# Cross-attention on one core: 64-row products in pairs, mask and maximum in one pass, longer load steps, last keys in 256 columns

## The chip, the cores and the metric

The kernel runs on one core of one Trainium2 chip. The metric is the device time of one execution in microseconds. The core has five engines with a queue each: TensorE (PE; PEld is its weight load), VectorE (DVE), ScalarE (ACT), GpSimd (POOL) and SyncE (SP), which here only issues DMAs. The engines wait for each other through semaphores.

## What is computed

Sixteen batches of 256 query rows attend to 77 keys each with 8 heads; then come an output projection, a residual and a layer norm. The reference, cut:

```python
Q = (img_embed @ Wq).reshape(B, -1, H, D).transpose(0, 2, 1, 3)     # B=16, 256 rows, H=8, D=256
K = (sent_embed @ Wk).reshape(B, -1, H, D).transpose(0, 2, 1, 3)    # 77 keys of 192 features
V = (sent_embed @ Wv).reshape(B, -1, H, D).transpose(0, 2, 1, 3)
score = jnp.einsum('bhqd,bhkd->bhqk', Q, K) / math.sqrt(D)
score = jnp.where(mask, score, -jnp.inf)
attn = jax.nn.softmax(score, axis=-1)
ctx = jnp.einsum('bhqk,bhkd->bqhd', attn, V).reshape(B, -1, H * D)
out = ctx @ Wo + img_embed
return (out - mu) * jax.lax.rsqrt(var + EPS) * gamma + beta
```

All inputs but the integer mask are 32-bit floats.

## The kernel before

**Folded weights.** The kernel multiplies the weights first: `gA` and `gB` hold Wq times Wk for each head, `uA` and `uB` hold Wv times Wo. The 192 features of the keys are split into 128 (the A part) and 64 (the B part). So each later product with the keys has two parts: A, a product over 128 rows, and B, over 64 rows, where two products can share the array, one in its upper and one in its lower half. Both parts add up in the same PSUM bank.

**Tiles.** A tile `t` is 128 query rows, so batch `b` has tiles 2b and 2b+1. Four batches (8 tiles) are a group `g`. x is held by group (`xg`), beside a copy `xT` whose 32 by 32 blocks VectorE turns after the load (L147 to L150).

**The loop.** `for b in range(-1, B - 1)` (L882 on) is software-pipelined: a pass works on the scores of batch b+1 and on the output of batch b, and finishes the norm of batch b-1. I call one turn of it a pass. In the order in which a pass is written:

- `scores` (L276) of the two new tiles: 128 products of 154 columns into four PSUM banks.
- `shift` (L292) of each: VectorE adds the mask's bias to the scores of eight heads (L298, two instructions) and takes the negative maximum per head (L305).
- `prepare_vw` (L198) makes batch b+1's keys times `uA`, `uB` in two banks `pv`; `prepare_a` (L153) makes one quarter of the next group's keys times `gA`, `gB` in four banks `pa`. All A parts are issued first (L208, L173), then all B parts (L219, L185). For the last group half of the batches are done at a time, with 154 columns instead of 308.
- `exponential` (L308): sixteen ACTIVATEs on ScalarE, one per head and tile, with the head's maximum as bias. `finish` takes the norm's statistics of an old tile. `weigh` (L315): VectorE sums the exponentials (L318) and inverts the sums (L320), POOL multiplies (L326) into `p`.
- ScalarE copies `pv` and `pa` from PSUM into `vw` and `a` (L922), POOL forms differences of `vw` (L379).
- `seven` (L402): seven block products instead of eight, in two banks `pm` and `po`, through `contract` (L413). The last 13 keys of each of the eight heads are a product of their own (`last`, L427), taken in columns of 128.
- VectorE normalises an old tile (L513, L532), turns the new `p` (L336), and on some passes `xT`. At the end of the pass come loads for the next group, `add_seven` (POOL and VectorE add the products to x) and `sums` (POOL, four additions on the turned `p` that the next `seven` uses).

From pass 13 on, `attend` (L343) takes the place of `seven`, and the last tiles are finished after the loop.

**What sets the order.** The kernel writes out the order of each engine's queue by hand (`manual_schedule`), so the order above is the order on each engine. All PSUM tiles share one ring of eight banks (`ps_mm`, `bufs=8`): the ninth tile asked for takes the bank of the first and waits for whoever reads that last. A pass asks for twelve: four for scores, two `pv`, four `pa`, two for `seven`. Each engine works its queue in order; an instruction that waits holds all behind it.

Of the kernel before, what the change touches and what calls it, by code (L numbers as in the profile page):

```python
# [1 line left out]

# [9 lines left out]
ALU = mybir.AluOpType  # L12
# [8 lines left out]
KM = 64  # L21
MASKED = 3.0e38


@with_exitstack
def kernel(
# [84 lines left out]

    def load_x(g):
        xg_of[g] = const.tile([P, GT, DI], F32, tag=f"xg{g}", name=f"xg_{g}")
        nc.sync.dma_start(xg_of[g], x_rows[:, g * GT : (g + 1) * GT, :])

# [36 lines left out]

    def prepare_a(g, places, lo=0, hi=GB):  # L153


        if 0 in places:
            a_of[g] = in_two("a", [P, 2, GB, H, S2], g)
        parts = [
            (2 * u + i, dc) for u in places for dc in range(2) for i in range(2)
        ]  # L160
        batches = slice(g * GB + lo, g * GB + hi)
        banks = [
            ps_mm.tile([P, hi - lo, S2], F32, tag="mm", name=f"pa_{g}_{h}_{dc}_{lo}")
            for h, dc in parts
        ]

        def cols(dc, i):
            return slice((2 * i + dc) * BK, (2 * i + dc + 1) * BK)

        def part_A():  # L170
            for (h, dc), o in zip(parts, banks):
                for i in range(NM):
                    nc.tensor.matmul(  # L173
                        flat(o[i * BK : (i + 1) * BK]),
                        gA[:, h, cols(dc, i)],
                        flat(cA[:, batches, :]),
                        start=True,
                        stop=False,
                    )

        def part_B():
            for j in range(0, len(parts), 2):
                for i in range(NM):
                    for k, (h, dc) in enumerate(parts[j : j + 2]):
                        nc.tensor.matmul(  # L185
                            flat(banks[j + k][i * BK : (i + 1) * BK]),
                            gB[half(k), h // 2, cols(dc, i)],
                            flat(cB[half(k), batches, :]),
                            start=False,
                            stop=True,  # L190
                        )

        def copies():
            return [(a_of[g][:, dc, lo:hi, h, :], o) for (h, dc), o in zip(parts, banks)]

        return part_A, part_B, copies

    def prepare_vw(b):  # L198

        vw_of[b] = vwp.tile([P, 4, 2, P], F32, tag="vw", name=f"vw_{b}", bufs=3)  # L200
        parts = slice(0, 4) if b < NS else slice(1, 5)
        pv = []

        def part_A():
            for k in range(2):
                pv.append(ps_mm.tile([P, 2 * DI], F32, tag="mm", name=f"pv_{b}_{k}"))
                for i in range(NM):
# [3 lines left out]
                        uA[:, parts, :, i],  # L211
                        start=True,
                        stop=False,
                    )

        def part_B():
            for i in range(NM):
                for k in range(2):
# [3 lines left out]
                        uB[half(k), parts, :, i],  # L222
                        start=False,
                        stop=True,
                    )
# [66 lines left out]
    def shift(t):  # L292
# [3 lines left out]
        s = sp.tile([P, H, S2], F32, tag="s", name=f"s_{t}")  # L296
        for a in range(2):
            nc.vector.tensor_tensor(  # L298
                s[:, a * H // 2 : (a + 1) * H // 2],
                ps[a][:, : H // 2 * S2].rearrange("p (h k) -> p h k", k=S2),  # L300
                bias[:, b, :].unsqueeze(1).to_broadcast([P, H // 2, S2]),
                ALU.add,
            )
        top = st.tile([P, H], F32, tag="top", name=f"top_{t}")
        nc.vector.tensor_reduce(top, s, AX.X, ALU.max, negate=True)  # L305
        s_of[t] = s, top

    def exponential(t):  # L308
        e = sp.tile([P, H, S2], F32, tag="e", name=f"e_{t}")
        s, top = s_of.pop(t)  # L310
        for h in range(H):
            nc.scalar.activation(e[:, h], s[:, h], AF.Exp, bias=top[:, h : h + 1])  # L312
        e_of[t] = e

    def weigh(t):  # L315
        e = e_of.pop(t)
        den = st.tile([P, H], F32, tag="den", name=f"den_{t}")
        nc.vector.tensor_reduce(den, e, AX.X, ALU.add)  # L318
        rden = st.tile([P, H], F32, tag="rden", name=f"rden_{t}")
# [82 lines left out]
    def seven(b):  # L402
# [7 lines left out]
        s1, s3, s2, s4 = (ss[:, i] for i in range(4))  # L410
        ends = vr[:, b, :P], vr[:, b, P:]

        def contract(out, *terms):  # L413
            for n, (weight, moving) in enumerate(terms):
                for i in range(NM):
# [3 lines left out]
                        moving,  # L419
                        start=(n == 0),  # L420
                        stop=(n == len(terms) - 1),
                    )
# [3 lines left out]

        last = [(pT[i][:, NF], vr[:, b, j * P : (j + 1) * P]) for i in range(QT) for j in range(2)]  # L427
        contract(pm[:, 0], *block(pT[0][:, 0:2], b11))
        contract(pm[:, 1], *block(s2, t2))
        contract(pm[:, 2], *block(s3, t3))  # L430
        contract(pm[:, 3], *block(s1, t1))
        contract(po[:, 0], *block(pT[0][:, 2:4], b21), last[0])
        contract(po[:, 1], *block(s4, b22), last[1])
        contract(po[:, 2], *block(pT[1][:, 2:4], t4), last[2])
        contract(po[:, 3], last[3])
        for i in range(QT):
# [441 lines left out]


    assert QT == 2  # L880
    last = NT - 1
    for b in range(-1, B - 1):  # L882
# [12 lines left out]
        for t in new:  # L895
            shift(t)
        for n in range(0, 2) if b < 0 else range(b + 2, min(b + 3, B // 2)):
            turn_last(n)
        g, n = (b + 1) // GB + 1, (b + 1) % GB
        work = [prepare_vw(b + 1)]  # L900
        if g < NG - 1 or g == NG - 1 and n < NF // 2:
            work.append(prepare_a(g, (n,)))
        elif b < NS:
            work.append(prepare_a(NG - 1, (NF // 2 + n % 2,), *((0, 2) if g < NG else (2, GB))))
        for part_A, _, _ in work:
            part_A()
        for _, part_B, _ in work:
            part_B()
        for i, t in enumerate(new):
# [3 lines left out]
            weigh(t)  # L913
        if old and b < B - 2:
            spread(old[0], old[-1] + 1)
        if b < 0:
            bias_of(GB, B)
            for j in range(GT // 2, GT, 2):
                transpose_x(0, j)
        for _, _, copies in work:  # L920
            for dst, src in copies():
                nc.scalar.copy(dst, src)  # L922
        if b + 1 < NS:
            differences(b + 1)
        if b < NS:
# [5 lines left out]
            for t in new:  # L931
                turn(t)
            if g < NG and n >= NF - 2:
                for j in range((n - NF + 2) * GT // 2, (n - NF + 3) * GT // 2, 2):
                    transpose_x(g, j)
            if old:
                normalise(old[1])


            if g < NG and n == NF - 1:  # L940
                load_x(g)
            elif g < NG and n:
                load_xT(g, (n - 1) * GT // 2, n * GT // 2)
            if now:
                add_seven(b)
            if b + 1 < NS:
                sums(b + 1)
# [73 lines left out]
```

## Time and profile before

| | us |
|---|---|
| median of 3 runs (274.39 to 274.52) | 274.43 |
| the profiled execution | 274.61 |
| its span, from first to last instruction | 272.8 |
| loop's scores begin on TensorE | 53.3 |
| TensorE's last product ends | 268.1 |
| one pass, batches 2 to 9 | 14.10 |
| busy in the pass 120.05 to 134.15: TensorE / VectorE / ScalarE / POOL | 14.10 / 11.86 / 7.65 / 10.94 |

The profiled execution is one execution, so differences are counted against its span; what lies outside the span is the same small amount in each. The chain of waits follows the last instruction back to whatever released it; a wait off that chain costs nothing until it becomes late. In rows of instructions, the number behind x is how many there are, and "mean ns" is how long one takes from its start to its end; neighbours on an engine may overlap, so the distance from start to start can be shorter. TensorE's products overlap too, and their ends are modelled: their starts are what to compare. A few rows of VectorE, ScalarE and POOL that the change touches:

```profile
L312 ACT ACTIVATE e<-s,top 128x77 f32<-128x77 f32 x256 | 66.8, 346 | 73.4 <-DVE top L305 73.4
L298 DVE TENSOR_TENSOR s<-ps,bias 128x308 f32<-128x308 f32 x64 | 29.7, 473 | 14.7 <-PE ps L283 14.6
L318 DVE TENSOR_REDUCE den<-e 128x8 f32<-128x616 f32 x32 | 24.9, 777 | 5.1 <-ACT e L312 4.9
L305 DVE TENSOR_REDUCE top<-s 128x8 f32<-128x616 f32 x32 | 25.4, 795 | 1.1
```

### The profile page before, as it was taken

What the parts mean: (1) busy time and instruction counts of PE and PEld (TensorE: products, weight loads), DVE (VectorE), ACT (ScalarE), POOL (GpSimd) and SP (SyncE); (2) the same over time, 40 slices, a digit from 0 to 9 for tenths busy, and PEclk for the clock granted to TensorE, in tenths of its full rate; (3) what the DMA queues carried; (4) which work ended last, traced back from release to release, by engine and by line L of the source; (5) the groups of instructions that cost most, each with busy time, mean ns of one, the idle gap of its engine ahead of it and who ended that gap; (6) DMA issues with size and microseconds to landing.
All of it is one profiled execution on the core that took longest, in us unless ns stands there. A gap on an engine that the chain in (4) does not pass through costs nothing.

```text
span 272.8 us, 14124 instructions
## 1 busy us (share of the span) xinstructions
PE 265.8 (97%) x6312; PEld 194.3 (71%) x6312; DVE 214.1 (78%) x418; ACT 136.2 (50%) x444; POOL 170.4 (62%) x231
## 2 busy tenths in 40 slices
PE   7999999999999999999999999999999999999992
PEld 6557486867494949495959586867796969694662
DVE  0554938589759898979799897878798989889875
ACT  3233225363918182827364646464546372927652
POOL 1000002809887878687878777777788789845754
PEclk9999999999999999999999999999999999999999
DMA  6999989940000322310221405000504061010102
GB/s 191 194 198 189 305 160 183 278 53 2 2 5 4 88 35 73 124 44 4 70 52 36 87 19 180 31 16 9 116 2 120 2 197 41 5 43 4 61 22 77
DMA packets 42460, 22.66 MB, mean 83 GB/s; under 512 B 23632, under 2 KB 41632, under 8 KB 42400
## 3 DMA queue, kind: packets, MB, share of 16 engines
q1 hardware_dynamic: 42400, 21.77, 34.8%
q8 instruction: 49, 0.80, 1.3%
q14 instruction: 11, 0.09, 0.1%
HBM read 17.57 MB, written 4.19 MB: 80 GB/s over the span
## 4 chain that ended last, share of the span: by engine, by line
PE 89%; DMA 7%; DVE 1%; SPq 1%; issue 0%; DVEq 0%
PE ps L283 25%; PE pa L173 11%; PE po L416 10%; PE pv L208 10%; PE pm L416 9%; PE pv L219 6%; PE pa L185 5%; DMA wq_blk<-in_L_xattn_Wq_dram 5%; PE po L348 4%; PE pu L717 3%; PE pr L242 2%; DMA c_sb<-in_ctx_dram 2%; PE pw L731 1%; PE pr L254 1%; PE po L364 1%; PE pgb L777 1%
## 5 line engine op out<-in xcount | busy, mean ns | idle before, releaser
L312 ACT ACTIVATE e<-s,top 128x77 f32<-128x77 f32 x256 | 66.8, 346 | 73.4 <-DVE top L305 73.4
L283 PE MATMUL ps<-a,xT 128*32 128x154 f32 x2048 | 70.0, 294 | 0.0
L326 POOL TENSOR_TENSOR p<-e,rden 128x512 f32<-128x512 f32 x64 | 47.8, 768 | 31.8 <-DVE rden L320 16.6
L283 PEld LDWEIGHTS ps<-a,xT 128*32 128x32 f32 x2048 | 66.0, 110 | 1.5 <-issue 0.8
L298 DVE TENSOR_TENSOR s<-ps,bias 128x308 f32<-128x308 f32 x64 | 29.7, 473 | 14.7 <-PE ps L283 14.6
L449 POOL TENSOR_TENSOR xg<-xg,m 128x256 f32<-128x256 f32 x39 | 28.6, 733 | 12.8 <-DVE xg L463 10.7
L173 PE MATMUL pa<-cA,gA 128*32 128x308 f32 (+1 forms) x576 | 36.4, 394 | 0.0
L173 PEld LDWEIGHTS pa<-cA,gA 128*32 128x32 f32 x576 | 18.4, 110 | 20.3 <-issue 9.1
L208 PE MATMUL pv<-uA,cA 128*32 128x512 f32 x256 | 30.4, 592 | 0.0
L318 DVE TENSOR_REDUCE den<-e 128x8 f32<-128x616 f32 x32 | 24.9, 777 | 5.1 <-ACT e L312 4.9
L305 DVE TENSOR_REDUCE top<-s 128x8 f32<-128x616 f32 x32 | 25.4, 795 | 1.1
L336 DVE STREAM_TRANSPOSE pT<-p 128x640 f32<-128x640 f32 x32 | 25.1, 813 | 0.9 <-POOL p L326 0.9
L379 POOL TENSOR_TENSOR ts<-vw 128x768 f32<-128x768 f32 x13 | 23.9, 1839 | 0.0
L532 DVE SCALAR_TENSOR_TENSOR xg<-xg,rstd,bet 128x256 f32<-128x256 f32 x26 | 20.9, 803 | 1.9
L185 PE MATMUL pa<-cB,gB 64*32 64x308 f32 (+1 forms) x576 | 20.3, 392 | 0.0
L922 ACT COPY vw<-pv 128x512 f32<-128x512 f32 x32 | 17.1, 584 | 6.3 <-PE pv L219 6.3
L185 PEld LDWEIGHTS pa<-cB,gB 64*32 64x32 f32 x576 | 10.7, 107 | 12.3 <-issue 9.2
L594 POOL COPY cRA<-cA 128x208 f32<-128x208 f32 x1 | 0.4, 358 | 29.8 <-DVE cA L593 29.8
L416 PE MATMUL po<-vr,pT 128*32 128x128 f32 x416 | 18.5, 273 | 0.0
L922 ACT COPY a<-pa 128x308 f32<-128x308 f32 (+1 forms) x56 | 17.5, 416 | 0.0
L219 PE MATMUL pv<-uB,cB 64*32 64x512 f32 x256 | 17.4, 601 | 0.0
L463 DVE TENSOR_TENSOR xg<-po,xg 128x256 f32<-128x256 f32 x31 | 11.7, 415 | 5.0 <-PE po L416 4.6
(117 smaller groups left out, 408.7 us busy)
## 6 DMA issues: line engine op xcount, KB each, us to landing
xT<-in_x_dram SPq DMA_DIRECT2D x32, 128.0 KB, 4.4
xg<-in_x_dram SPq DMA_DIRECT2D x4, 1024.0 KB, 6.7
out_dram<-xg SPq DMA_DIRECT2D x11, 256.0 KB, 2.8
wo<-in_L_xattn_Wo_dram SPq DMA_DIRECT2D x4, 512.0 KB, 6.2
wq_blk<-in_L_xattn_Wq_dram SPq DMA_DIRECT2D x12, 128.0 KB, 4.7
wvT<-in_L_xattn_Wv_dram SPq DMA_DIRECT2D x16, 96.0 KB, 3.6
out_dram<-xg SPq DMA_DIRECT2D x10, 128.0 KB, 1.7
wk_blk<-in_L_xattn_Wk_dram SPq DMA_DIRECT2D x12, 96.0 KB, 4.6
```

Of the source, the lines that this page charges most:

```text
L173: nc.tensor.matmul(flat(o[i * BK : (i + 1) * BK]), gA[:, h, cols(dc, i)], flat(cA[:, batches, :]), start=True, stop=False,)
L185: nc.tensor.matmul(flat(banks[j + k][i * BK : (i + 1) * BK]), gB[half(k), h // 2, cols(dc, i)], flat(cB[half(k), batches, :]), start=False ...
L208: nc.tensor.matmul(pv[k][i * BK : (i + 1) * BK], cA[:, b, k * BK : (k + 1) * BK], uA[:, parts, :, i], start=True, stop=False,)
L219: nc.tensor.matmul(pv[k][i * BK : (i + 1) * BK], cB[half(k), b, k * BK : (k + 1) * BK], uB[half(k), parts, :, i], start=False, stop=True,)
L283: nc.tensor.matmul(ps[m // 2][i * BK : (i + 1) * BK, m % 2 * 2 * S2 : (m % 2 + 1) * 2 * S2], xT_of[g][:, j * NM + m, dc], flat(a_of[g][:, ...
L298: nc.vector.tensor_tensor(s[:, a * H // 2 : (a + 1) * H // 2], ps[a][:, : H // 2 * S2].rearrange("p (h k) -> p h k", k=S2), bias[:, b, :]. ...
L305: nc.vector.tensor_reduce(top, s, AX.X, ALU.max, negate=True)
L312: nc.scalar.activation(e[:, h], s[:, h], AF.Exp, bias=top[:, h : h + 1])
L326: nc.gpsimd.tensor_tensor(part, e_mh[:, :, :, keys], rden_mh.unsqueeze(3).to_broadcast(list(part.shape)), ALU.mult,)
L416: nc.tensor.matmul(out[i * BK : (i + 1) * BK], weight[:, i], moving, start=(n == 0), stop=(n == len(terms) - 1),)
L449: nc.gpsimd.tensor_tensor(to, to, what, ALU.add)
L922: nc.scalar.copy(dst, src)
```

## The change

Five edits are made together.

1. **64-row products in pairs.** For batches 0 to 11, two batches' preparations are issued in one pass (those with b+1 even): A and B of the first, then, after ScalarE's copies of the first in the program's order, B and A of the second. The next pass issues none. To this end the start and stop flags of the accumulation can be swapped (`rest_first`). Batches 12 to 15 are prepared one a pass, as before. For the half-group preparations two `pa` now share a bank.
2. **Mask and maximum in one pass.** `shift` becomes one instruction per head that adds the bias, writes the negated sum and its minimum; the exponential gets the scale -1. For the first 26 tiles ScalarE's exponential also gives the sum over the keys (`accum_out`), and VectorE's sum L318 is left out.
3. **Loads.** x and its turned copy are loaded in steps of four tiles at the head of passes with n even; before, x came in one step of eight tiles and the turned copy in two of four at the ends of passes.
4. **Order.** Turning xT and normalising the second old tile are put off, in the passes without preparation, to after the next pass's `shift`. In the passes with two, `sums` goes ahead of `add_seven`. In pass -1, turning the rest of group 0's xT and the bias of batches 4 to 15 move behind the turn of `p`.
5. **Last keys.** Their product is taken first in each half of `po`, in 256 columns.

```diff
-    def prepare_a(g, places, lo=0, hi=GB):
+    def prepare_a(g, places, lo=0, hi=GB, rest_first=False):
...
+        opening, closing = range(len(whole)), range(len(parts) - len(whole), len(parts))
...
-                        start=True,
-                        stop=False,
+                        start=not rest_first and n in opening,
+                        stop=rest_first and n in closing,
...
-        for a in range(2):
-            nc.vector.tensor_tensor(
-                s[:, a * H // 2 : (a + 1) * H // 2],
-                ps[a][:, : H // 2 * S2].rearrange("p (h k) -> p h k", k=S2),
-                bias[:, b, :].unsqueeze(1).to_broadcast([P, H // 2, S2]),
-                ALU.add,
+        top = st.tile([P, H], F32, tag="top", name=f"top_{t}")
+        for h in range(H):
+            a, k = divmod(h, H // 2)
+            nc.vector.tensor_tensor_reduce(
+                s[:, h],
+                ps[a][:, k * S2 : (k + 1) * S2],
+                bias[:, b, :],
+                scale=-1.0,
+                scalar=FAR,
+                op0=ALU.add,
+                op1=ALU.min,
+                accum_out=top[:, h : h + 1],
             )
-        top = st.tile([P, H], F32, tag="top", name=f"top_{t}")
-        nc.vector.tensor_reduce(top, s, AX.X, ALU.max, negate=True)
...
-            nc.scalar.activation(e[:, h], s[:, h], AF.Exp, bias=top[:, h : h + 1])
+            one = slice(h, h + 1)
+            nc.scalar.activation(
+                e[:, h],
+                s[:, h],
+                AF.Exp,
+                bias=top[:, one],
+                scale=-1.0,
+                accum_out=den[:, one] if t < QT * NS else None,
+            )
...
-        nc.vector.tensor_reduce(den, e, AX.X, ALU.add)
+        if t >= QT * NS:
+            nc.vector.tensor_reduce(den, e, AX.X, ALU.add)
...
-        contract(po[:, 0], *block(pT[0][:, 2:4], b21), last[0])
-        contract(po[:, 1], *block(s4, b22), last[1])
-        contract(po[:, 2], *block(pT[1][:, 2:4], t4), last[2])
-        contract(po[:, 3], last[3])
+        for i in range(QT):
+            contract(flat(po[:, 2 * i : 2 * i + 2]), (pT[i][:, NF], vr[:, b, :]), final=False)
+            if i == 0:
+                contract(po[:, 0], *block(pT[0][:, 2:4], b21), first=False, final=False)
+                contract(po[:, 1], *block(s4, b22), first=False)
+            else:
+                contract(po[:, 2], *block(pT[1][:, 2:4], t4), first=False)
...
+    def work_of(b, rest_first=False):
+        g, n = b // GB + 1, b % GB
+        work = [prepare_vw(b, rest_first)]
+        if g < NG - 1 or g == NG - 1 and n < NF // 2:
+            work.append(prepare_a(g, (n,), rest_first=rest_first))
+        elif b <= NS:
+            part = (0, 2) if g < NG else (2, GB)
+            work.append(prepare_a(NG - 1, (NF // 2 + n % 2,), *part, rest_first))
+        return work
...
+        while behind:
+            behind.pop(0)()
         g, n = (b + 1) // GB + 1, (b + 1) % GB
...
+        if g < NG and n % 2 == 0:
+            load_x(g, n, 2 * QT)
+            load_xT(g, n * QT, (n + 2) * QT)
...
+        alone = b + 1 >= B - GB
+        works = work_of(b + 1) if alone or n % 2 == 0 else []
...
+        ahead = works and not alone
...
+        if ahead:
+            copy_out(works)
+            if old:
+                spread(old[0], old[-1] + 1)
+            works = work_of(b + 2, rest_first=True)
+            for _, part_B, _ in works:
+                part_B()
+            for part_A, _, _ in works:
+                part_A()
+        copy_out(works)
...
+            if alone or ahead:
+                turn_x_and_normalise(g, n, old)
+            else:
+                behind.append(partial(turn_x_and_normalise, g, n, old))
+            if ahead:
+                sums(b + 1)
             if now:
                 add_seven(b)
-            if b + 1 < NS:
+            if b + 1 < NS and not ahead:
                 sums(b + 1)
```

## The prediction, on record before the changed kernel ran

> **What bounds the kernel now.** I read the page's busy times first, then the shares of the chain that ended last, then that chain in order of time, and last the timeline of one steady pass.
>
> ```profile
> PE 265.8 (97%) x6312; PEld 194.3 (71%) x6312; DVE 214.1 (78%) x418; ACT 136.2 (50%) x444; POOL 170.4 (62%) x231
> PE 89%; DMA 7%; DVE 1%; SPq 1%; issue 0%; DVEq 0%
> ```
>
> TensorE is the bound: from 24.2 us to 268 us the chain never leaves it. One pass of the loop, in the chain (start, length, what):
>
> ```profile
> 120.05 4.19 PE ps L283 x128
> 124.24 1.72 PE pv L208 x16
> 125.95 2.07 PE pa L173 x32
> 128.03 1.02 PE pv L219 x16
> 129.05 1.04 PE pa L185 x32
> 130.08 1.89 PE pm L416 x64
> 131.97 2.18 PE po L416 x80
> 134.15 0.90 PE ps L283 x25
> ```
>
> The pieces touch: 14.10 us a pass, with no wait in it. So only two things move the time: TensorE's own work, and a wait that becomes late enough to hold it. The other engines in that pass, from the timeline:
>
> ```profile
> 120.12 0.76 DVE L463 TENSOR_TENSOR xg<-po,xg 128x256 f32<-128x256 f32 x2 [0.64 <-PE po L416]
> 121.17 0.48 DVE L298 TENSOR_TENSOR s<-ps,bias 128x308 f32<-128x308 f32 x1 [0.29 <-PE ps L283]
> 124.82 0.80 DVE L305 TENSOR_REDUCE top<-s 128x8 f32<-128x616 f32 x1
> 123.62 4.20 ACT L312 ACTIVATE e<-s,top 128x77 f32<-128x77 f32 x16 [5.04 <-DVE top L305]
> 127.82 3.08 POOL L326 TENSOR_TENSOR p<-e,rden 128x512 f32<-128x512 f32 x4 [1.83 <-ACT e L312]
> 129.14 1.07 ACT L922 COPY vw<-pv 128x512 f32<-128x512 f32 x2 [0.39 <-PE pv L219]
> 130.10 1.40 ACT L922 COPY a<-pa 128x308 f32<-128x308 f32 x4
> ```
>
> The reader is to see that ScalarE's sixteen exponentials stand, in its queue, ahead of the copies that free the PSUM banks, and that these copies have almost a whole pass of room today. The starts of TensorE's groups show what a change of shape costs:
>
> ```profile
> 125.77 2.25 PE L173 MATMUL pa<-cA,gA 128*32 128x308 f32 x32
> 127.96 1.09 PE L219 MATMUL pv<-uB,cB 64*32 64x512 f32 x16
> 128.84 1.24 PE L185 MATMUL pa<-cB,gB 64*32 64x308 f32 x32
> 130.01 0.64 PE L416 MATMUL pm<-vw,pT 128*32 128x128 f32 x16
> ```
>
> The 128-row `pa` takes 2.19 us from its start to the next group's, though 32 such products need 2.06; the 64-row `pa` takes 1.17 where 32 of them need 1.04 (the chain's 2.07 and 1.04). About 0.13 us is lost on entering the 64-row shape and 0.13 on leaving it.
>
> **The skill.** TensorEngine Tiling (Array Packing), section Key Properties, says that a change of tiling mode drains the array; the two gaps of 0.13 us agree. VectorE: DVE Perf Modes, section "Two Vector instructions with no wait between them", says that an operation which also writes out its accumulator is two instructions; nothing in this trace uses one. Perfetto Trace Analysis, section Optimizing Scalar/DVE Operations, gives some 60 ns (SBUF) or 125 ns (PSUM) of access per VectorE instruction and 93 ns per ScalarE instruction on SBUF. The trace agrees roughly: of two L298 back to back (0.82 us for two of 473 ns) the second starts 0.35 us after the first, 308 elements being 0.31 at the 1.0 ns an element of rows L463 and L481 (415 - 288 ns over 128).
>
> **Part by part, on TensorE.** *Pairs.* Today each batch enters and leaves the 64-row shape once. For batches 0 to 11 the order becomes A, B, B, A: six pairs, each without one leaving and one entering: 6 x 0.26 = 1.56 us gained. The products themselves stay. *Last keys.* 416 products of 128 columns become 208 of 256. A product of 128 columns takes 27.3 ns (2.18 us / 80), and the columns alone, from the 512-column row (1.72 / 16 / 4 = 26.9), nearly all of it. So 8 starts fewer a batch at 0.5 to 2.5 ns, 13 batches: 0.05 to 0.26 us; I take 0.1. TensorE gains 1.65 us.
>
> **Loads.** x of groups 1 to 3 comes in 6 transfers instead of 3, its turned copy in the same 24, now at the head of even passes instead of the tail. SP issues them before that pass's stores; a reload of xT waits only for scores that ended a pass earlier, and each half is turned two passes after its load. The chain has no DMA after 24 us: nothing, either way. The moved bias and xT work of pass -1 (VectorE 0.69 + 1.12 + 1.29, POOL 2.2 us) now precedes the first `sums`, due at 73.7 us; I get its third sum at about 71.5.
>
> **Vector and scalar work.** Let T be VectorE's time for one head (one pass and its accumulator's read) and E ScalarE's for one exponential with a sum. Before: a tile costs 2 x 473 + 795 ns for mask and maximum, and 777 for the sum. After: 8T, and no sum for tiles 0 to 25. T lies between 0.20 (80 ns of elements, 60 access, 60 read) and 0.45 (237 ns from the slope of L463's and L481's rows, plus a whole 128x1 TENSOR_SCALAR, 209). I take 0.25: the instructions overlap, and the smallest ones here, the BATCH_NORM_AGGREGATE, follow at 0.10. E is 0.262 today (4.20 / 16). Its read costs from nothing (kept in the same instruction) to 0.204 (the smallest ACTIVATE here, rstd). I take 93 ns of access: E = 0.356.
>
> **The wait that takes the place of room.** A pair of passes is now uneven. The long one holds both batches' preparation (19.8 us), the short one only scores and `seven` (8.1). Eight PSUM banks are not enough for two preparations, so the second one's 64-row `pa` waits for the first one's copies by ScalarE, which stand behind the sixteen exponentials. Clock from the long pass's scores:
> - TensorE: scores to 4.18, A to 8.09, B to 10.01, second `pv` to 10.89, first half of the second 64-row `pa` to 11.41. There it needs two `a` copies.
> - VectorE comes late out of the short pass. There `shift` starts 1.30 after the scores (121.17 - 119.87), that is at 21.06 of the pair, and takes 16T; then vr, statistics and the reciprocal 1.34, four `p` on POOL 3.08, the second turn 0.81, the product's add 0.76. The next long pass begins at 27.87, so its `shift` starts at 16T - 0.82: 3.2 for T = 0.25, against 1.30 today.
> - ScalarE: first exponential T + 0.06 later, 16E, two vw copies 1.07, two `a` copies 0.70.
>
> TensorE is held by S = 17T + 16E - 10.4 us when that is positive. With T = 0.25 and E = 0.356, S = -0.45: no stall, but thin. Behind the waiting products stand the second A part and `seven`; nothing makes the loss good, since the next pair starts its clock at TensorE. It can occur in the passes of batches 2, 4, 6 and 8: pass -1 has no short pass before it, and batches 10 and 11 use half as many banks. The other waits (`top` for the banks, vw's) come later than these only for T above 0.35. One loss I charge: before pass 11, `sums` stands behind add_seven on POOL, and its third sum lands some 0.2 to 0.3 us after TensorE wants it.
>
> Sum: -1.56 - 0.1 + 0.2 = -1.45 us. The profiled execution took 274.61 us with a span of 272.8, 0.18 above the median 274.43; 274.61 - 1.45 = 273.2 for it, and 273.0 for the median.
>
> **Rivals.** (1) *ScalarE's sum is dear.* One mechanism: the read behind each exponential delays the copies, and TensorE stalls four times. It decides from S = 0.36 (four times that is the gain), at T = 0.25 from E = 0.407, a read of 145 ns. With the rstd row's 204 ns, S = 1.31, 5.2 us lost: 278.2, slower. For it: ScalarE works in order, so every read delays all behind it. Against: its exponentials overlap today, 262 ns apart against 346 long. (2) *VectorE's head is dear.* T of 0.34 gives S = 1.1 and 277.4; at 0.45, 32T plus 14.3 us of other work exceeds the pair's 27.9, near 286. Against: two long sums go, and short instructions overlap here. (3) *Little is gained*: a stall of 0.2 to 0.4 us a pair, or a drain that is also paid between batches: 273.9 to 274.9, taken as 274.4.
>
> **Numbers.** Forecast without stall 0.56; rival 1 0.21; rival 2 0.13; rival 3 0.10. A change of under 0.2% (0.55 us) can't be told from none. Faster 0.56, same 0.10, slower 0.34. Alone, the forecast reaches from 272.3 (no wait before pass 11, last keys at 0.26) to 273.8. The range takes in rival 3 and rival 1 up to about its price: 272.2 to 279.0.
>
> **What would show it.** Right: pv L219 to pa L185 twice in a row without a gap, pairs near 27.9 us, TensorE's idle time as small as now. Wrong: idle time ahead of the second 64-row `pa`, ended by ScalarE's vw or a copies; exponentials over 0.40 apart; sixteen heads over 4.8 us.

## The result and the profile after

The changed kernel takes 272.63 us (median of 16 executions, 271.95 to 276.73); the kernel before takes 274.55 us beside it (16 executions, 273.96 to 276.42). The ratio is 0.9935, with a 95% interval of 0.9916 to 0.9955, which is 1.2 to 2.3 us. The ratios here and below are of fast runs alone; one run of the changed kernel (276.73) and one of e7 count as slow and are left out of them. The forecast was 273.0.

The page of the changed kernel, first its busy times, then the shares of the chain of waits:

```profile
PE 265.1 (97%) x6104; PEld 191.6 (70%) x6104; DVE 187.4 (69%) x808; ACT 155.7 (57%) x652; POOL 171.4 (63%) x231
PE 81%; SPq 8%; DMA 7%; DVE 2%; issue 1%; DVEq 0%
```

TensorE has 208 instructions fewer, VectorE 26.7 us less work and ScalarE 19.5 us more. TensorE is still the bound inside the loop; its share of the chain fell only because the chain of this execution reaches TensorE later (SyncE's queue and loads hold it up to then). One pair of passes, in the chain of waits of the changed kernel, in order of time (start, length, what):

```profile
106.88 4.19 PE ps L289 x128
111.07 1.72 PE pv L214 x16
112.79 2.07 PE pa L180 x32
114.86 1.02 PE pv L225 x16
115.88 1.04 PE pa L192 x32
116.91 0.86 PE pv L225 x16
117.77 1.04 PE pa L192 x32
118.81 1.85 PE pv L214 x16
120.66 2.07 PE pa L180 x32
122.74 1.75 PE pm L434 x64
124.48 2.17 PE po L434 x64
126.66 4.19 PE ps L289 x128
130.84 1.75 PE pm L434 x64
132.59 2.17 PE po L434 x64
134.76 4.19 PE ps L289 x128
```

The pieces touch again, and the second 64-row `pa` (117.77) waits for nothing. The pair takes 134.76 - 106.88 = 27.88 us, against 28.20 for two passes of the kernel before. The difference can be read piece by piece. The second `pv` L225 takes 0.86 where the first takes 1.02: 0.16 us for entering the 64-row shape is paid once, not twice. Both `pm` take 1.75 instead of 1.89, and `pv` L214 behind the B parts 1.85 instead of 1.72: leaving the shape costs 0.13 to 0.14, and it too is paid once. The two `po` are 0.01 shorter each.

Where the whole gain sits. I compare the time from the scores of batch 2 to the end of the last VectorE instruction, since it leaves out how late the loop began in each execution: 77.75 to 270.06 = 192.31 us before, 79.00 to 269.67 = 190.67 after, so -1.64. Four pairs give 4 x 0.32 = 1.28; the pair of batches 10 and 11, with half a group's preparation, takes 24.84 instead of 25.19, another 0.35: together 1.63. The first pair adds 0.31 where nothing disturbs it (24.10 against 24.41, as in runs e5 and e8 below). That makes 1.94, against 1.92 between the two medians. That these two agree so closely is luck, since the interval of the ratio reaches from 1.2 to 2.3 us; the trace is the better witness.

The profiled execution itself took 274.03 us (span 272.2), 1.4 over the median: its loop began at 54.27 instead of 53.34, and the A part of its first pass took 2.71 us instead of 2.07. Its steady passes are those of the list above.

The rows of groups on the page of the changed kernel that answer to the rows of VectorE and ScalarE before:

```profile
L324 ACT ACTIVATE e<-s,top 128x77 f32<-128x77 f32 x256 | 83.8, 346 | 44.8 <-DVE top L306 41.8
L306 DVE CUSTOM_DVE_ANT_0 s<-ps,bias 128x77 f32<-128x77 f32 x256 | 43.8, 232 | 13.6 <-PE ps L289 13.6
L324 ACT ACTIVATION_READ_ACCUMULATOR e<-s,top 128x1 f32 x208 | 39.0, 188 | 0.0
L306 DVE DVE_READ_ACCUMULATOR2_ANT top<- 128x1 f32 x256 | 20.8, 81 | 0.0
```

Each accumulator has a row of its own, on both engines, as the Trainium skill says for VectorE (VectorE: DVE Perf Modes, section "Two Vector instructions with no wait between them"). But 232 + 81 ns and 346 + 188 ns are not what these pairs cost. The timeline of the changed kernel, of VectorE and of ScalarE, shows the distance from start to start:

```profile
127.94 0.23 DVE L306 CUSTOM_DVE_ANT_0 s<-ps,bias 128x77 f32<-128x77 f32 x1
128.09 0.08 DVE L306 DVE_READ_ACCUMULATOR2_ANT top<- 128x1 f32 x1
128.09 0.23 DVE L306 CUSTOM_DVE_ANT_0 s<-ps,bias 128x77 f32<-128x77 f32 x1
...
128.47 0.34 ACT L324 ACTIVATE e<-s,top 128x77 f32<-128x77 f32 x1
128.72 0.19 ACT L324 ACTIVATION_READ_ACCUMULATOR e<-s,top 128x1 f32 x1
128.81 0.34 ACT L324 ACTIVATE e<-s,top 128x77 f32<-128x77 f32 x1
```

Two heads on VectorE begin 0.15 to 0.16 us apart: T = 0.158 over the sixteen heads of a long pass. Two exponentials with a sum begin 0.343 apart, and sixteen take 5.50 us, so E = 5.50 / 16 = 0.344, where the prediction had 4.20 / 16 = 0.262 without a sum. From start to start the exponentials without a sum are closer than that, because 4.20 / 16 holds the end of the last one and a longer step between the two tiles: in the changed kernel's late tiles, which have no sum, sixteen take 4.11 us, that is (4.11 - 0.35) / 15 = 0.250. So the read's row is 188 ns long and moves the next exponential by 93.

How near the long pass is to a stall, in the timeline of the changed kernel (ScalarE's copies, then TensorE's second 64-row products):

```profile
143.85 1.07 ACT L913 COPY vw<-pv 128x512 f32<-128x512 f32 x2 [0.37 <-PE pv L225]
144.81 1.40 ACT L913 COPY a<-pa 128x308 f32<-128x308 f32 x4
...
144.59 1.06 PE L225 MATMUL pv<-uB,cB 64*32 64x512 f32 x16
145.45 1.24 PE L192 MATMUL pa<-cB,gB 64*32 64x308 f32 x32
```

The bracket says that ScalarE stood idle for 0.37 us ahead of its copies, waiting for TensorE: its exponentials were done. Two `a` copies are done at 144.81 + 0.70 = 145.51, and the second half of the 64-row `pa` needs them at 145.45 + 0.52 = 145.97. So the exponentials could end 0.37 + 0.46 = 0.83 us later before TensorE is held.

In the short pass ahead of it there is hardly any. VectorE's timeline of the changed kernel, at the end of a short pass:

```profile
161.62 0.20 DVE L339 RECIPROCAL rden<-den 128x8 f32<-128x8 f32 x1 [0.95 <-ACT e L324]
161.74 0.43 DVE L533 SCALAR_TENSOR_TENSOR xg<-xg,mv,gam 128x256 f32<-128x256 f32 x1
162.28 1.09 DVE L552 SCALAR_TENSOR_TENSOR xg<-xg,rstd,bet 128x256 f32<-128x256 f32 x1
163.29 1.56 DVE L355 STREAM_TRANSPOSE pT<-p 128x640 f32<-128x640 f32 x2
164.78 0.71 DVE L483 TENSOR_TENSOR xg<-po,xg 128x256 f32<-128x256 f32 x2
```

The second reciprocal waits for the exponentials' sums, and from there to the `shift` of the long pass, which follows the last line, VectorE has no gap. So the end of the short pass's exponentials sets the `shift`, to within 0.03 us (e5 and e6 measure this). Ahead of the long passes of batches 4 and 6 VectorE does wait 0.5 us in this stretch, for POOL's `p`; but `p` comes from the same reciprocal, and the `shift` begins just as long after the scores there.

### The profile page after: what moved, and what is told of

Same layout as the page of the kernel before. It is cut to its first block, busy times and chain, and to the rows that moved or that the text cites. A ratio compares the mean times of both kernels' runs of the same rounds, so it can differ in the third digit from the quotient of the medians.

```text
span 272.2 us, 14362 instructions
## 1 busy us (share of the span) xinstructions
PE 265.1 (97%) x6104; PEld 191.6 (70%) x6104; DVE 187.4 (69%) x808; ACT 155.7 (57%) x652; POOL 171.4 (63%) x231
## 4 chain that ended last, share of the span: by engine, by line
PE 81%; SPq 8%; DMA 7%; DVE 2%; issue 1%; DVEq 0%
PE ps L289 25%; PE pv L214 10%; PE po L434 10%; PE pa L180 9%; PE pm L434 8%; PE pv L225 6%; DMA wq_blk<-in_L_xattn_Wq_dram 5%; PE pa L192 5%; PE po L367 4%; SPq L596 3%; SPq L607 3%; DMA cB<-in_ctx_dram 1%; PE pr L248 1%; DVE uB L878 1%; PE pr L260 1%; SPq L640 1%
## 5 line engine op out<-in xcount | busy, mean ns | idle before, releaser
L324 ACT ACTIVATE e<-s,top 128x77 f32<-128x77 f32 x256 | 83.8, 346 | 44.8 <-DVE top L306 41.8
L306 DVE CUSTOM_DVE_ANT_0 s<-ps,bias 128x77 f32<-128x77 f32 x256 | 43.8, 232 | 13.6 <-PE ps L289 13.6
L324 ACT ACTIVATION_READ_ACCUMULATOR e<-s,top 128x1 f32 x208 | 39.0, 188 | 0.0
L180 PE MATMUL pa<-cA,gA 128*32 128x308 f32 (+1 forms) x576 | 37.0, 394 | 0.0
L214 PE MATMUL pv<-uA,cA 128*32 128x512 f32 x256 | 30.5, 594 | 0.0
L355 DVE STREAM_TRANSPOSE pT<-p 128x640 f32<-128x640 f32 x32 | 25.8, 824 | 4.1 <-POOL p L345 4.0
L913 ACT COPY vw<-pv 128x512 f32<-128x512 f32 x32 | 17.7, 584 | 12.7 <-PE pv L214 7.9
L306 DVE DVE_READ_ACCUMULATOR2_ANT top<- 128x1 f32 x256 | 20.8, 81 | 0.0
L913 ACT COPY a<-pa 128x308 f32<-128x308 f32 (+1 forms) x56 | 18.9, 399 | 1.7 <-PE pa L180 0.2
L225 PE MATMUL pv<-uB,cB 64*32 64x512 f32 x256 | 17.3, 597 | 0.0
L533 DVE SCALAR_TENSOR_TENSOR xg<-xg,mv,gam 128x256 f32<-128x256 f32 x27 | 16.7, 618 | 0.1
```

Of the source, the lines that this page charges most:

```text
L180: nc.tensor.matmul(flat(o[i * BK : (i + 1) * BK]), gA[:, h, cols(dc, i)], flat(cA[:, batches, :]), start=not rest_first and n in opening, ...
L214: nc.tensor.matmul(pv[k][i * BK : (i + 1) * BK], cA[:, b, k * BK : (k + 1) * BK], uA[:, parts, :, i], start=not rest_first, stop=rest_first,)
L225: nc.tensor.matmul(pv[k][i * BK : (i + 1) * BK], cB[half(k), b, k * BK : (k + 1) * BK], uB[half(k), parts, :, i], start=rest_first, stop=n ...
L306: nc.vector.tensor_tensor_reduce(s[:, h], ps[a][:, k * S2 : (k + 1) * S2], bias[:, b, :], scale=-1.0, scalar=FAR, op0=ALU.add, op1=ALU.min ...
L324: nc.scalar.activation(e[:, h], s[:, h], AF.Exp, bias=top[:, one], scale=-1.0, accum_out=den[:, one] if t < QT * NS else None,)
L355: nc.vector.transpose(pT_of[t].rearrange("p n m q -> p m n q"), p.rearrange("p m (n k) -> p m n k", k=BK),)
```

## The experiments

The theory: six pairs save changes of shape on TensorE, and the vector and scalar work earns nothing by itself but keeps the copies early enough. The rivals: the pairs alone would have done it; the gain comes from the vector work; or the room is much larger or smaller than I worked out. Every time below stands beside a run of the kernel before on the same chip. Two parts of the fourth edit have no run of their own: `sums` ahead of `add_seven`, and the work moved in pass -1.

The medians of nearly equal kernels still scatter by up to 1 us between groups of runs, and the profiled executions show one reason: the loop's first scores begin at 52.8 to 54.3 us, and the first pair is delayed by 0 to 1.4. So e10 and e11, whose traces differ from the changed kernel's by 0.13 us and less, have medians of 273.61 and 272.85. For small differences I therefore use the distance of starts inside the trace, and name it "loop to end": from the scores of batch 2 to the end of the last VectorE instruction, 192.31 before and 190.67 after.

| run | median, us | ratio to before (95%) | pairs of batches 2, 4, 6, 8 in the trace, us | loop to end, us |
|---|---|---|---|---|
| e1: new vector work, no pairs | 275.48 | 1.0032 (1.0012 to 1.0051) | 2 x 14.10 | 192.85 |
| e2: pairs, all vector work old | 278.96 | 1.0141 (1.0112 to 1.0171) | 28.29, 28.76, 28.76, 28.51 | 196.45 |
| e3: pairs, new shift, VectorE's sums | 273.65 | 0.9966 (0.9948 to 0.9984) | 27.88 | 191.00 |
| e4: pairs, old shift, ScalarE's sums | 290.08 | 1.0551 (1.0505 to 1.0597) | 29.91, 32.21, 30.56, 30.55 | 207.6 |
| e5: ScalarE slower by half a read | 273.88 | 0.9973 (0.9962 to 0.9984) | 27.88, 28.41, 28.39, 28.40 | 192.57 |
| e6: ScalarE slower by a read | 283.26 | 1.0321 (1.0295 to 1.0348) | 29.25, then 29.88 | 201.7 |
| e7: norm not put off | 276.75 | 1.0081 (1.0051 to 1.0111) | 27.88, 28.86, 28.85, 28.45 | 194.11 |
| e8: a seventh pair | 273.85 | 0.9975 (0.9954 to 0.9996) | 27.88 | 191.13 |
| e9: loads as before | 273.91 | 0.9961 (0.9943 to 0.9979) | 27.88, 28.94, 27.99, 27.88 | 191.83 |
| e10: last keys as before | 273.61 | 0.9966 (0.9948 to 0.9985) | 27.90 | 190.80 |
| e11: all sums on ScalarE | 272.85 | 0.9919 (0.9895 to 0.9944) | 27.88 | 190.75 |
| e12: e8 and e11 together | 273.97 | 0.9960 (0.9942 to 0.9977) | 27.88 | 190.85 |

**e1, the vector work without the pairs.** The kernel before, with the new `shift` and ScalarE's sums only.

```diff
-            nc.vector.tensor_tensor(s[:, a * H // 2 : (a + 1) * H // 2], ...
-        nc.vector.tensor_reduce(top, s, AX.X, ALU.max, negate=True)
+            nc.vector.tensor_tensor_reduce(s[:, h], ..., accum_out=top[:, h : h + 1])
...
+                accum_out=den[:, one] if t < QT * NS else None,
```

> The kernel before with only the new shift (one instruction a head) and the sum taken by ScalarE; no pairs, old loads, old last keys. Theory (only TensorE's changes of shape were worth anything; the vector edits merely keep a wait away): 274.5 us like before, passes of 14.10 us, though VectorE is some 3 us a pass less busy. Rival (the relief of VectorE is itself the gain): 273.5 us or less.

Passes stayed at 14.10 us; the kernel is slightly slower. Loop to end is 0.54 longer, most of it in one pass (215.58 to 228.64 = 13.06 us instead of 12.60), in which `seven` stood still for 0.25 us and the profile shows no releaser. VectorE's 24 us less buy nothing here: they were all hidden.

**e2, the pairs without the vector work.** The changed kernel with the old `shift` and VectorE's sums.

```diff
-            nc.vector.tensor_tensor_reduce(s[:, h], ...
+            nc.vector.tensor_tensor(s[:, a * H // 2 : (a + 1) * H // 2], ...
+        nc.vector.tensor_reduce(top, s, AX.X, ALU.max, negate=True)
...
+        nc.vector.tensor_reduce(den, e, AX.X, ALU.add)
```

> The changed kernel with the old shift and the sum back on VectorE; pairs, loads and last keys stay. Theory: the short pass hands VectorE on about 1.5 us later and the first exponential waits for a whole tile's maximum, so the copies come about 0.8 us too late in each of four long passes: 272.6 + 3.1 = 275.7 us (274.6 to 276.5), TensorE idle ahead of the second 64-row pa. Rival (the edits simply add up, the pairs are worth 1.9 us whatever VectorE does): 272.6 us.

The stall is where it was expected, and in the four long passes together not larger; but beyond 212 us the chain leaves TensorE altogether. The chain of waits of e2, at the second 64-row `pa` of a long pass:

```profile
116.70 0.48 ACT vw L900
117.22 1.85 PE pa L192 x31
```

TensorE goes on only when ScalarE's `vw` copy is done, and 31 of the 32 products come after it. Two pairs take 28.76, so each loses 0.88, close to the 0.8 expected; the other two lose 0.41 and 0.63, all four together 2.8 where 3.1 was expected. The time is nevertheless 2.5 us above the expected range: loop to end is 5.8 longer than in the changed kernel, and the rest, 3.0, is lost behind the four pairs, where nothing had been expected: 0.4 in the pair of batches 10 and 11, 1.3 in the passes of batches 12 and 13, and 1.3 at the end. The pairs without the vector work make the kernel slower; the vector work is what lets them pay.

**e3, which half of the vector work.** New `shift`, but every sum on VectorE.

```diff
-                accum_out=den[:, one] if t < QT * NS else None,
+                accum_out=None,
...
-        if t >= QT * NS:
-            nc.vector.tensor_reduce(den, e, AX.X, ALU.add)
+        nc.vector.tensor_reduce(den, e, AX.X, ALU.add)
```

> The changed kernel with every sum over keys back on VectorE, new shift kept. Theory: VectorE is 1.6 us a pass busier and the long pass's shift starts later, but sixteen exponentials without their reads are 1.3 us shorter: no stall, 272.6 us (272.3 to 273.2). Rival (ScalarE's sum is needed for the gain): 274 us or more.

No pair changes: 27.88. What is lost, 0.33 in loop to end, is lost at one place, in pass 11 (from the scores of pass 10 to those of pass 12, 206.55 to 227.57 = 21.02 us, against 20.70). The median, 273.65, lies 0.45 above the expected range. The chain of waits of e3 there:

```profile
223.08 0.75 POOL ss L416
223.88 1.52 PE pm L433 x48
```

`seven` waits for the third of POOL's sums, which stood behind `add_seven`. This is the wait for which the prediction charged 0.2; it is not there in the changed kernel, where the third sum ends at 223.95 and is needed at 224.29, and appears in e3 and e5, where VectorE is later in the passes around it. So the pairs don't need ScalarE's sum; it is worth this wait.

**e4, the other half.** Old `shift`, ScalarE's sums kept.

```diff
-            nc.vector.tensor_tensor_reduce(s[:, h], ...
+            nc.vector.tensor_tensor(s[:, a * H // 2 : (a + 1) * H // 2], ...
+        nc.vector.tensor_reduce(top, s, AX.X, ALU.max, negate=True)
...
-                scale=-1.0,
                 accum_out=den[:, one] if t < QT * NS else None,
```

> The changed kernel with the old shift (two additions and one maximum a tile), sum kept on ScalarE. Theory: exponentials start 1.7 us later behind a whole tile's maximum and are still 0.344 us apart, so the stall is the largest of the four mixtures, about 1.3 us in each of four long passes: 277.6 us (276 to 279). Rival (additive edits): 272.6 us.

The direction was right, the size far off (276 to 279 expected): two pairs lose 2.7 us, the others 2.0 and 4.3, and 27% of the chain are exponentials. The exponentials were expected to start 1.7 us later. They start 6.66 us after the scores of a long pass instead of 3.13, 3.53 later: 2.1 because the `shift` itself starts later, the rest behind a whole tile's maximum. Less the room of 0.83 that is 2.70, near the 2.7 of two pairs; in the pair that loses 4.3 one group of 128-row products (`pv` L214) takes 3.27 us instead of 1.85, and the trace does not show why. The late `shift` and the longer exponentials add up, and the new `shift` is the part that the pairs can't do without: e2 and e4 stall without it, e3 with it does not.

**e5 and e6, the price of ScalarE.** An idle one-column ACTIVATE on ScalarE, which nobody reads, behind every second (e5) or every (e6) exponential of the first 26 tiles. Each moves what follows by 0.093 us, so E rises by 0.046 on the average (e5) and by 0.093 (e6).

```diff
+    spare = const.tile([P, 1], F32, tag="spare", name="spare")
...
+            for _ in range((t < QT * NS) * (h % 2)):        # e6: range(1 if t < QT * NS else 0)
+                nc.scalar.activation(spare, eps, AF.Identity)
```

> The changed kernel with one idle ScalarE instruction of one column behind every second exponential of tiles 0 to 25: nothing else changes, an exponential takes on average some 0.05 us longer. Theory (the copies have 0.8 us of room in a long pass, and sixteen times 0.05 uses it up): no or hardly a stall, 272.6 to 273.3 us. Rival (ScalarE is already at its limit, every added step shows): 13 batches of 0.8 us give 280 us or more.

> The same with one idle instruction behind each exponential, some 0.09 us. Theory: 1.5 us later in the long pass, and 0.7 us more because the short pass's exponentials also hold back the norm and the turns in front of the next shift: stall 1.4 us in each of four long passes, 278 us (276 to 281). Rival (ScalarE is only 57% busy, so 1.5 us a pass more hides): 272.6 us.

Both medians lie above the expected range, 273.88 by 0.6 and 283.26 by 2.3. e5 shows the threshold. In three of the four long passes a pair takes about 28.4 (in the one of batch 2, whose short pass has no norm of an older batch yet, nothing is lost), and the second 64-row `pa` 1.56 us instead of 1.04, in the chain of waits of e5:

```profile
116.00 1.56 PE pa L193 x31
```

e6 shows the slope: 2.00 us in three pairs, 1.37 in that of batch 2. Its chain of waits runs through both passes of the pair:

```profile
106.42 0.35 ACT e L325 x2
107.00 0.36 DVE xg L536
107.45 1.09 DVE xg L555
108.54 1.48 DVE pT L358 x2
110.02 0.64 DVE xg L486 x2
...
117.99 0.48 ACT vw L916
118.51 1.85 PE pa L193 x31
```

The reader is to see the first five lines as one chain: the exponentials of the short pass release VectorE's second reciprocal (0.20 us, not among the lines) and then the norm L536, behind which VectorE has in its queue the rest of the norm, the turns of `p`, the product's add and then the `shift` of the long pass. The exponentials of the long pass come on top. So a slower exponential is paid 32 times in a pair, not 16. The `shift` of the long pass starts 10.90 us after the short pass's scores in the changed kernel, 11.52 in e5 and 12.26 in e6: 0.62 and 1.36 later, where the sixteen exponentials of the short pass, from the first's start to the last's, became 0.65 and 1.39 longer: hardly any room there. In the long pass the copies stand behind 8 and 16 idle instructions, 0.74 and 1.48 us, and have the 0.83 of room worked out above: 0.62 + 0.74 - 0.83 = 0.53 (measured 0.52 at the `pa`), and 1.36 + 1.48 - 0.83 = 2.01 (measured 2.00).

**e7, the norm not put off.** The second norm stays in the short pass. (Only the norm is at stake: the code turns `xT` at even n alone, so the passes without preparation have no turn of `xT` to put off.)

```diff
-            if alone or ahead:
-                turn_x_and_normalise(g, n, old)
-            else:
-                behind.append(partial(turn_x_and_normalise, g, n, old))
+            turn_x_and_normalise(g, n, old)
```

> The changed kernel with the second old tile's norm done at the end of the short pass again instead of after the next shift. Theory: the long pass's shift starts 1.0 us later, which is just over the room of 0.8 us: stall 0.2 us in four passes, 273.3 us (272.6 to 274.0). Rival (the order of the norm does not matter): 272.6 us.

The pairs of batches 4 and 6 lose 0.98 and 0.97 us, that of batch 8 loses 0.57, and that of batch 2, which has no older norm ahead of it, nothing. The median, 276.75, is far above the 272.6 to 274.0 expected. The chain of waits of e7 has the second norm ahead of the `shift`:

```profile
107.62 1.20 DVE xg L533
108.85 0.56 DVE xg L552
```

These two steps take 1.76 us, and the `shift` of the long pass starts 12.72 us after the short pass's scores instead of 10.90, 1.82 later; less the room of 0.83 that is 0.99, where 0.98 was measured. Ahead of batch 8 the `shift` is 1.44 late, which gives 0.61 (measured 0.57). I had counted only about 1 us for the norm. This one place in VectorE's queue is thus worth three times what a pair gains.

The stalls of e2 and e4 to e7 fit one clock. Counted from the scores of the long pass of batch 6, ScalarE's first copy starts at 9.09 us in the changed kernel, where it waits for TensorE. It starts at 10.34 in e2, 12.14 in e4, 9.97 in e5, 11.46 in e6 and 10.44 in e7, and each pair loses what that is beyond 9.46, the one number fitted here: 0.88, 2.68, 0.51, 2.00 and 0.98. Whatever is slowed down, it is the lateness of this copy that TensorE pays.

**e8, e11 and e12, can more be had?** e8 prepares batches 12 and 13 as a seventh pair; e11 takes all sums on ScalarE; e12 does both.

```diff
-        alone = b + 1 >= B - GB
+        alone = b + 1 >= B - 2                              # e8, e12
...
-                accum_out=den[:, one] if t < QT * NS else None,
+                accum_out=den[:, one],                      # e11, e12, and no sum L337
```

> The changed kernel with batches 12 and 13 prepared as a seventh pair. Theory: one round of changes of shape less, 0.3 us as for each of the six pairs: 272.3 us. Rival (the late passes have less room, because half preparations make them short, and the sum on VectorE comes back at tile 26): a stall eats it, 272.6 us or more.

> The changed kernel with the sum taken by ScalarE's exponential in all 32 tiles, not only in the first 26; VectorE's 6 remaining sums (about 0.78 us each) are gone. Theory (the end of the kernel is TensorE's and the sums of the last tiles have cover): 272.6, no change (272.2 to 273.0). Rival (at the end VectorE decides, so six sums fewer are worth something): 271.5 to 272.2. The opposite (at the end ScalarE is the one with less room: 48 reads at 0.08 us): up to 273.5.

> As the seventh pair (batches 12 and 13 prepared together), and in addition all sums by ScalarE. Theory (the seventh pair gives 0.3 us on TensorE and loses it again because VectorE decides the end, with the sums of tiles 26 to 31 in its chain): with these sums gone it keeps the gain, 272.2 us (271.5 to 272.5), and beats the changed kernel. Rival (the late chain is bound by the shift's eight instructions a tile and by the norm, not by these sums): as the seventh pair alone, 273.5 to 274.1, the chain from 234 us on still VectorE's.

The seventh pair does its part on TensorE: batches 12 and 13 take 24.84 us instead of 25.17, so 0.33 is gained once more. In e8 the loop is TensorE's to 234.65 us; from there the chain of waits is VectorE's, with its sums in it:

```profile
230.39 4.23 PE ps L289 x128
234.65 0.24 DVE s L306
...
235.92 0.69 DVE den L337
```

Loop to end is 0.46 longer than in the changed kernel: more than the pair gained is given back, as the rival had it. e11 leaves the end as it was (190.75 against 190.67), so six sums fewer are worth nothing by themselves. e12, expected at 272.2, came out at 273.97, in its rival's range. It takes back part of e8's loss (190.85), but still gains nothing: from 232.10 us its chain runs through the exponentials and VectorE to the end. So the sums were one part of that late chain, and the exponentials and the `shift` the rest. None of the three beats the changed kernel.

**e9, the loads where they were.**

```diff
-        if g < NG and n % 2 == 0:
-            load_x(g, n, 2 * QT)
-            load_xT(g, n * QT, (n + 2) * QT)
...
+            if g < NG and n == NF - 1:
+                load_x(g, 0, GT)
+            elif g < NG and n:
+                load_xT(g, (n - 1) * GT // 2, n * GT // 2)
```

> The changed kernel with the loads of x and its turned copy back where they were (one step of eight tiles, and the turned copy at the ends of passes). My step (the loads are worth nothing, the chain has no DMA after 24 us): no difference from the changed kernel, 272.6 us (272.2 to 273.1), pairs of passes 27.88. Rival (the longer and earlier steps hide a wait that the new order would otherwise have): an idle time of TensorE or of VectorE at the turning of xT, ended by a load, in the pairs of batches 0 to 9, and 273.2 or more.

This one is not settled. The median, 273.91, lies above the expected range, in the rival's; but three of the four pairs take 27.88 to 27.99, and no wait in the loop is ended by a load. One pair takes 28.94, with this in the chain of waits of e9:

```profile
105.95 0.50 PE ps L289 x11
106.45 0.62 issue
```

TensorE stops within a group of products, and the profile has no releaser for it. The loads of that stretch were over by then (no packet moved from 105 to 107 us). Such stops of TensorE are in other runs too, where the loads are the new ones (0.73 us at 60.05 in e12, 1.06 at 60.56 in e4, both in the first pass), so this one can't be put down to the loads; nor can it be excluded that they have a part in it. Without that pair's 1.06 us, loop to end would be 190.77, as in the changed kernel.

**e10, the last keys in 128 columns.**

```diff
-            contract(flat(po[:, 2 * i : 2 * i + 2]), (pT[i][:, NF], vr[:, b, :]), final=False)
+        contract(po[:, 0], *block(pT[0][:, 2:4], b21), last[0])
+        contract(po[:, 1], *block(s4, b22), last[1])
```

> The changed kernel with the last keys' product in columns of 128 again. My step (8 starts fewer a batch, 0.1 us in all, bounds 0.05 to 0.26): 272.7 us (272.5 to 273.0), the group po 2.18 us long instead of 2.17, pairs of passes 27.89 to 27.92. Rival (the 256 columns bring nothing or cost): 272.6 or less and pairs no longer than 27.88.

In the trace it is what was expected: `po` 2.18 us again, pairs 27.90, loop to end 0.13 longer. The median of 273.61 lies above the expected range by 0.6; nothing in the steady passes accounts for that, and I leave it open.

## Why the prediction was right, point by point

**The bound and the likeliest case: right.** TensorE carries the loop, no long pass stalls, and the time is TensorE's own gain: 1.92 us measured, 1.45 forecast.

**The switch: mechanism right, size a little small.** The term was 6 x 0.26 = 1.56. Entering measured 0.16 and leaving 0.14, so 0.30 a pair (e10, with the last keys as before, has it alone: 28.20 - 27.90), 1.80 in six. The forecast had read these gaps between starts of groups; the pairs give them directly. That a change of shape costs TensorE time agrees with the Trainium skill, TensorEngine Tiling (Array Packing), section Key Properties; that the cost is a drain of the array, as it says there, no run here shows by itself.

**Last keys: right in size, with a slip in the count.** 0.1 forecast, 0.13 measured. The forecast counted 8 starts fewer a batch; the `po` lines have 64 products instead of 80, so it is 16, at 0.6 ns each (0.01 us / 16).

**The charge of 0.2 before pass 11: not paid.** The wait is real (e3, e5), but in the changed kernel POOL's third sum is in time. That and the switch term, 0.2 + 0.24, are nearly all of the 0.47 between forecast and result, as far as the medians can tell.

**ScalarE's exponential with a sum: right, its base a little long.** E was taken as 0.356, which is 0.262 and the price of an access in the Trainium skill's Perfetto Trace Analysis, section Optimizing Scalar/DVE Operations (93 ns). The read moved the next exponential by just these 93 ns; but the base from start to start is 0.250, not 0.262, and so E is 0.344. That the page's price of an access is also that of this read was a guess that came true.

**VectorE's head: outside the bounds.** T was taken as 0.25, with 0.20 as the lower end; it is 0.158. The lower bound added the page's access time and a read to the elements; in fact the read and the next head run beside each other, and 77 elements at 1.0 ns leave 80 ns for all the rest.

**The stall's formula: the clock of the long pass nearly right, its slopes wrong.** It put the `shift` of the long pass at 3.2 us after the scores; it began at 137.56 - 134.76 = 2.80. With the measured T the formula gives 16 x 0.158 - 0.82 = 1.7, so that 3.2 came near 2.80 was luck. It doesn't hold for so small a T: the heads of the short pass come bank by bank, as TensorE delivers the scores (the last bank's at 130.91, 4.25 after the scores began). Worse, it counted ScalarE once a pair (16E). The path through reciprocal, norm, turn and `shift` counts it a second time (e5, e6). The stall-free forecast stood because the measured E leaves 0.83 us in the long pass; but by e5 and e6 the edge lies, as an estimate, at E = 0.344 + (0.83 + 0.03) / 32 = 0.371, not at 0.384, where the forecast's S would turn positive.

**Rival 1: right in kind, far too cheap.** It gave 278.2 us for E = 0.466. e6, at about 0.436, already takes 283.3. The range up to 279.0 would have been too narrow for it. Rival 2 is excluded by T, but e2 and e4 show that a late `shift` has the price that it feared. Rival 3 fell: each pair keeps its gain.

**Loads: nothing, as far as the runs tell;** e9's one stop of TensorE leaves that open.

## What to carry to other kernels

Where the bound engine has no gaps, look for what it pays between its instructions: here a change of product shape costs 0.30 us for going there and back, and putting two such stretches together saves one of them. What such a regrouping costs is found on the engines with room: write the clock of the now uneven stage for each of them, and follow a delay through every queue that it passes, since one slow kind of instruction can stand in the same path twice. An edit that is worth nothing by itself (e1) can be what makes another one pay (e2).

## What was unexpected of the hardware

A row's length is not its price. An accumulator's read on ScalarE has a row of 188 ns and moves its successor by 93; on VectorE a head with mask, negation, minimum and its accumulator's read has rows of 232 and 81 ns, and heads follow each other every 158 ns. For the same 616 elements the old way takes 473 x 2 + 795 = 1,741 ns by its rows, but from start to start 1.59 us (e2, two tiles without a wait between them: 221.94 and 223.53), and eight heads of the new take 8 x 158 = 1,264 ns, so the new `shift` saves about 0.33 us a tile. Most of what it is worth lies elsewhere: the first exponential starts 0.33 us after the `shift` begins, against 1.77 in e2.
